# The output product of later units by seven block products for eight, their gathers moved behind it, and the clearing of one tile opened to two engines

## The chip, the cores and the metric

The kernel runs on one core of a Trainium2 chip. The metric is the device time of one execution in microseconds; a kernel's time is the median of its runs. Five engines work side by side, each through its own queue in order: TensorE (PE; its weight loads are PEld), VectorE (DVE), ScalarE (ACT), GpSimd (POOL) and SyncE (SP), which here only issues DMAs.

## The reference, cut to what matters

For each of two batches, 2048 tokens `x` (640 wide) attend to 124 text tokens (8 heads of 80), and a second branch attends through 4 adapter tokens. Both results are added, multiplied by `Wout`, and the residual is added:

```python
hs = _mha(query, keyt, valt)                       # text attention, 124 keys
ca_q1 = jnp.einsum('btc,th->bch', ca, Wq_ca)[:, indices, :]
ca_hs1 = _mha(ca_q1, residual, residual)           # 384 distinct queries over all 2048 tokens
ca_hs2 = _mha(ca_hs1 @ Wq, ca_k2, ca_v2)           # 4 keys
out = (hs + ca_hs2) @ Wout + b_out + residual
```

`indices` repeats 384 rows over the 2048 tokens, so the second branch is computed for 384 rows only and looked up.

## The kernel before, in words

**A planner.** The body is written as generators that yield `Do(engine, fn, after, needs, frees, marks, rank)`. `Desk.run` (L122) keeps a clock for every engine, takes the operation that can start first (by its rank where several can), calls its function, which emits the instructions, and adds costs of its own. So the program's order on every engine is what this planner found. `Room` objects are counted buffers: `banks` (PSUM), `slots` (big SBUF slots), `rows` (tiles for residual rows), `ebs`, `es`, `ht2`, `ht1`, `pTs`. All arithmetic goes through a few helpers, so the profile's lines are mostly L165 (matmul), L175 (transpose), L186 (VectorE, ScalarE, GpSimd) and L206 (DMA by SP); tiles tell the groups apart.

**The work.** Tokens come in 32 tiles of 128; a unit `m` is two tiles, so there are 16 units, eight a batch.

- *Queries* (`pq`): x by Wq, 8 blocks of 512 tokens.
- *Adapter, first part* (`adapter`, L1158): per batch 24 sets of scores `s1` (tiles `s`), each reduced to maxima by one long VectorE instruction into `mx`. Then a tile `mt` is cleared on POOL (L1198), the maxima of `mx` are reduced into it, transposed by PE (`pm`), added to `ca0` and split into `cop`. With `cop` known, 32 more sets of scores (`s`) follow, each with an exponential on ScalarE (`ea`) and a contraction on PE (`acc`).
- *Adapter, second part* (`second`, L1293): from `acc` to `o2`, 384 rows of 640 in HBM per batch: the second branch, already multiplied by Wout and with the bias.
- *Text scores and softmax* (`text_scores` L1402, `softmax` L1435): per tile, scores `sc`, maxima `m`, differences into `p`, exponential, sum `r`, quotient (on POOL or VectorE), a 32x32 transpose `eb` on VectorE, and a store to HBM (`kept`).
- *Output of a unit* (`probabilities` L1490, `text_out` L1590): four loads bring the probabilities back with keys on partitions (`pT`); PE multiplies them by the values (`ph`, in three groups: head parts 0 and 1, 2 and 3, the rest), ScalarE or VectorE copies them out (`hsT` or `ht_more`, five chunks of 128 rows by 256 tokens), and PE multiplies them by `Wout`: for each of two tiles and each half of the 640 columns, five products of 128x128 by 128x320 into one bank `po`. So a unit has 20 products. `added` (L1666) adds `po` to the row tile (`xo` or `x_more`), which holds the residual.
- *Rows* (`residual` L1560, `add_second` L1580): the residual rows are loaded into a row tile. If `o2` is known when they are loaded, a gather on POOL adds the rows of `o2` at once, ahead of the unit's products; otherwise (`early`) the gather comes behind the adds; and if `o2` is still unknown there, the sum is stored to HBM, loaded again later (`xp`, `x_more`) and gathered then. A gather is an indirect DMA with an add; POOL writes its descriptors.

**Spare room.** When the last queries are done, `spread_out` (L1519) gives the big slots that came free to new buffers: a second `pT`, two more `eb`, more `hsT` (`ht_more`), two more probability tiles `p_more`, four more row tiles (`x_more`).

**Matmul records.** A product of float32 operands shows as two records in the profile: the 640 records of `po` are 16 units of 20 products.

Of the kernel before, what the change touches and what calls it, by code (L numbers as in the profile page):

```python
# [212 lines left out]
def kernel(  # L213
# [944 lines left out]
    def adapter(b):  # L1158
# [36 lines left out]
        both, at = op.value, op.slots[0][0]  # L1195
        mt = both[:, :2].rearrange("p j (a k) -> p a j k", a=NCC)
        less = both[:, 2:]
        yield Do("POOL", lambda: desk.g_memset(mt, 0.0))  # L1198

        def spread():  # L1200
            for k in (MAX, MAX + 1):
# [190 lines left out]

    kept_of, xr_of, early = {}, {}, {}

    def tiles(m):

# [91 lines left out]
    def probabilities(m):  # L1490

# [26 lines left out]

    def spread_out():  # L1519

        op = yield Do("NONE", lambda z: z[0], [("q", len(blocks) - 1)], needs=[(slots, 1)])
        spare["pT"] = op.value
        pTs.at.append(op.at.t)

        def more_eb(z):
            t = slot(z[0], "eb_more", [P, 2, 4 * HEADS * R])
            more_of.append(t.rearrange("p z (j h a) -> p z j h a", j=4, h=HEADS))

        op = yield Do("NONE", more_eb, [("q", len(blocks) - 1)], needs=[(slots, 1)])
        ebs.at += [op.at.t] * 2  # L1530

        def another_ht(z):
            t = slot(z[0], "ht_more", [P, 5 * 2 * P])
            more_ht[2] = [t[:, 4 * P * i : 4 * P * (i + 1)] for i in range(2)]
            more_ht[1] = [t[:, 8 * P :]]

        op = yield Do("NONE", another_ht, [("q", len(blocks) - 1)], needs=[(slots, 1)])
        ht2.at += [op.at.t] * 2
        ht1.at += [op.at.t]
        op = yield Do(  # L1540
            "NONE", lambda z: slot(z[0], "p_more", [P, 2, HEADS, NTOK]), [("q", len(blocks) - 1)], needs=[(slots, 1)]
        )
        more = op.value

        def clear():
            for i in range(2):
                desk.g_memset(more[:, i, :, NK:], 0.0)
                late["e"].append(more[:, i])

        op = yield Do("POOL", clear)  # L1550
        es.at += [op.at.t] * 2
# [6 lines left out]
        rows.at += [op.at.t] * 4  # L1558

    def residual(m):  # L1560

        xr = xr_of[m] = []
        for b, st in tiles(m):

            def load(at):
                t = x_tile(at[0], f"xo_{b}_{st}")
                dma(t, x[b, st * P : (st + 1) * P, :], 1.3)
                return t

# [20 lines left out]
    def text_out(m):  # L1590

        N = 2 * P
        b = tiles(m)[0][0]
        rank = lambda: 30 + m if desk.known(("o2", b)) else 60 + m
        for c0, n in ((0, 2), (2, 2), (4, 1)):

            def product(s, z, c0=c0, n=n):
                pT = pT_of[m]
                ph = bank(s[0], f"ph_{m}_{c0}")
                for k in range(n):  # L1600
                    for h in (2 * (c0 + k), 2 * (c0 + k) + 1) if c0 < 4 else ():
                        half = slice(VH * (h % 2), VH * (h % 2 + 1))
                        matmul(
                            ph[half, k * N : (k + 1) * N], vpad[b][:, h, :VH],
                            pT[:, :, :, h, :].rearrange("p i k a -> p k i a"),
                            start=True, stop=True, skip_group_check=True,
                        )
                for h in (0, 2, 4, 6, 1, 3, 5, 7) if c0 == 4 else ():
                    part = slice(R * (h // 2), R * (h // 2 + 1))
                    matmul(  # L1610
                        ph[part, :N], vpad[b][:, h, VH:],
                        pT[:, :, :, h, :].rearrange("p i k a -> p k i a"),
                        start=(h % 2 == 0), stop=(h % 2 == 1), skip_group_check=True,
                    )
                return ph

            room = ht2 if n == 2 else ht1
            op = yield Do(
                "PE", product, [("pT", m), "v done"], needs=[(banks, 1), (room, 1)],
                frees=[(pTs, room_of["pT", m])] if c0 == 4 else [],  # L1620
                mode=(P, 64 if c0 < 4 else 32), rank=rank,
            )
            room_of["hsT", m, c0] = room, op.slots[1][0]

            def out_of(ph=op.value, z=op.slots[1][0], n=n, c0=c0):
                if z >= 2:
                    t = more_ht[n][z - 2]
                else:
                    t = late["pool"].tile([P, n * N], F32, tag=f"ht{n}{z}", name=f"hsT_{m}_{c0}")
# [33 lines left out]

    hs_of = {}

    def added(m, k, u, po, s, at):  # L1666

        b, st = tiles(m)[k]
# [27 lines left out]
        if early[m]:  # L1696
# [70 lines left out]
```

## Time and profile before

| | us |
|---|---|
| time, median of 3 runs | 666.96 (666.58 to 667.25) |
| the profiled execution's own time | 666.84 |
| its span, first to last instruction | 665.1 |
| TensorE busy | 640.8 |
| VectorE busy | 395.0 |
| ScalarE busy | 207.8 |
| GpSimd busy | 119.2 |

How to read the lines below. A group line has the line of code, engine, operation, output <- input, shapes, count, then busy us and mean ns of one, then the idle time of the engine ahead of these instructions and what ended it. A timeline line has start, length, engine, what, and in brackets the idle time ahead of it and its releaser. The chain of waits is followed back from the last instruction. A DMA line has the size of one and the median time from issue to landing. Busy spans of PE overlap, since matmuls are pipelined: for what one costs, count a long run of them. In the table by stretches a bracket behind a busy time is the number of instructions.

### The profile page before, as it was taken

How to read it: one execution, taken by the hardware profiler on the slowest of the kernel's cores; microseconds unless marked ns; L12 is line 12 of the kernel's file. 1: busy time of each engine (PE TensorE's matmuls, PEld its weight loads, DVE VectorE, ACT ScalarE, POOL GpSimd, SP SyncE). 2: the span in 40 equal slices, each digit the busy share in tenths (PEclk: the TensorE clock that was granted, in tenths of full speed). 3: DMA queues.
4: the chain of work that ended last, by engine and by line, in shares of the span. 5: the costliest groups of instructions: out<-in, count | busy, mean ns of one | idle time of the engine just before them, and what ended most of it. 6: DMA issues, size and time to landing. Idle time of an engine off the chain costs nothing.

```text
span 665.1 us, 9016 instructions
## 1 busy us (share of the span) xinstructions
PE 640.8 (96%) x3547; PEld 319.6 (48%) x3547; DVE 395.0 (59%) x556; ACT 207.8 (31%) x264; POOL 119.2 (18%) x174
## 2 busy tenths in 40 slices
PE   6999999999999999999998999969999999999997
PEld 4555443344453433334444455544444456665665
DVE  2368999999998756978999999621010031111111
ACT  2221322322125665524332321105655632101010
POOL 7120101202026010001201108232020000126030
PEclk9999999999999999999999999969999999999999
DMA  8898359468274335231245288999191138599981
GB/s 271 144 235 117 72 159 226 122 165 166 79 163 97 131 98 109 89 102 33 83 124 162 90 199 218 256 251 228 49 248 43 45 98 203 203 228 276 284 235 59
DMA packets 135556, 102.39 MB, mean 154 GB/s; under 512 B 78293, under 2 KB 107349, under 8 KB 135514
## 3 DMA queue, kind: packets, MB, share of 16 engines
q1 hardware_dynamic: 129882, 91.13, 52.3%
q0 software_dynamic: 5632, 10.69, 8.8%
q8 instruction: 28, 0.46, 0.3%
q14 instruction: 14, 0.11, 0.1%
HBM read 64.30 MB, written 37.49 MB: 153 GB/s over the span
## 4 chain that ended last, share of the span: by engine, by line
PE 72%; DVE 20%; issue 3%; DMA 2%; POOL 1%; SPq 1%; ACT 0%; DVEq 0%; POOLq 0%
PE po L165 24%; PE pq L165 20%; PE acc L165 7%; PE ph L165 5%; DVE mx L186 5%; PE s L165 5%; PE sc L165 5%; DVE r L186 3%; DVE m L186 3%; DVE p L186 2%; DVE eb L186 2%; PE pyz L165 2%; DMA out_dram<-xo 2%; PE pk L165 1%; PE pv L165 1%
## 5 line engine op out<-in xcount | busy, mean ns | idle before, releaser
L165 PE MATMUL pq<-xt,wq_sb 128*128 128x512 f32 x320 | 154.6, 609 | 1.8 <-DVE p L186 0.8
L186 ACT ACTIVATE ea<-s 128x1536 f32<-128x1536 f32 x64 | 92.8, 1450 | 95.2 <-PE s L165 95.2
L165 PE MATMUL po<-wout_sb,hsT 128*128 128x320 f32 x376 | 119.2, 447 | 0.5 <-ACT hsT L186 0.5
L186 DVE TENSOR_REDUCE mx<-s 128x4 f32<-128x2048 f32 x48 | 109.1, 2273 | 7.0 <-PE s L165 6.7
L165 PEld LDWEIGHTS pq<-xt,wq_sb 128*128 128x128 f32 x320 | 55.7, 189 | 72.9 <-issue 70.6
L165 PEld LDWEIGHTS po<-wout_sb,hsT 128*128 128x128 f32 x376 | 69.8, 193 | 42.0 <-issue 17.1
L186 POOL TENSOR_TENSOR p<-p,r 128x992 f32<-128x992 f32 x19 | 35.4, 1861 | 282.5 <-DVE r L186 282.5
L165 PE MATMUL po<-wout_sb,ht_more 128*128 128x320 f32 x264 | 83.8, 442 | 0.0
L186 DVE TENSOR_TENSOR xo<-xo,po 128x320 f32<-128x320 f32 x36 | 17.3, 481 | 95.0 <-PE po L165 95.0
L186 DVE TENSOR_TENSOR x_more<-x_more,po 128x320 f32<-128x320 f32 x28 | 13.6, 486 | 89.7 <-PE po L165 89.7
L165 PEld LDWEIGHTS po<-wout_sb,ht_more 128*128 128x128 f32 x264 | 48.2, 190 | 29.9 <-issue 7.8
L165 PE MATMUL acc<-ea,y_sb 128*32 128x384 f32 x512 | 54.6, 498 | 0.0
L186 ACT ACTIVATE p<-p 128x992 f32<-128x992 f32 (+1 forms) x32 | 31.5, 985 | 65.8 <-DVE p L186 65.6
L1582 POOL DMA_INDIRECT x_more<-o,query x17 | 26.2, 1542 | 140.9 <-DMA x_more<-early 87.8
L165 PE MATMUL ph<-pT,vpad 128*32 128x256 f32 (+1 forms) x512 | 48.9, 386 | 1.1 <-issue 0.7
L186 DVE TENSOR_REDUCE m<-sc 128x4 f32<-128x496 f32 x64 | 42.0, 657 | 12.6 <-PE sc L165 12.6
L186 DVE TENSOR_TENSOR p<-sc,m 128x496 f32<-128x496 f32 x60 | 40.5, 674 | 2.1
L165 PEld LDWEIGHTS sc<-kmain,q 64*128 64x128 f32 x512 | 31.5, 187 | 17.3 <-issue 15.3
L165 PE MATMUL pq<-xt,wq 128*128 128x512 f32 x80 | 39.6, 609 | 0.0
L186 DVE TENSOR_REDUCE r<-p 128x8 f32<-128x992 f32 (+1 forms) x32 | 35.7, 1116 | 5.8 <-ACT p L186 5.8
L186 ACT COPY q<-pq 128x512 f32<-128x512 f32 x34 | 19.8, 584 | 58.2 <-PE pq L165 58.2
L165 PE MATMUL sc<-kmain,q 64*128 64x124 f32 x512 | 37.1, 284 | 0.0
(175 smaller groups left out, 566.6 us busy)
## 6 DMA issues: line engine op xcount, KB each, us to landing
pT<-kept SPq DMA_DIRECT2D x64, 256.0 KB, 7.2
kept<-eb SPq DMA_DIRECT2D x28, 512.0 KB, 3.5
xi<-in_x_dram SPq DMA_DIRECT2D x28, 256.0 KB, 4.6
xo<-in_x_dram SPq DMA_DIRECT2D x18, 320.0 KB, 7.5
out_dram<-x_more SPq DMA_DIRECT2D x17, 320.0 KB, 2.5
x_more<-in_x_dram SPq DMA_DIRECT2D x14, 320.0 KB, 6.6
out_dram<-xo SPq DMA_DIRECT2D x13, 320.0 KB, 5.9
y<-yt SPq DMA_DIRECT2D x16, 256.0 KB, 2.9
```

What stands on the lines that cost most here:

```text
L165: self.pin(self.nc.tensor.matmul(out, lhsT, rhs, **kw))
L186: self.pin(getattr(engine, what)(*args, **kw))
L1582: desk.pin(nc.gpsimd.indirect_dma_start(out=t, out_offset=None, in_=o2_of[b], in_offset=bass.IndirectOffsetOnAxis(ap=query[:, st : st + 1] ...
```

## The change

Three edits, of which the first two hang together.

1. **Seven block products.** From the unit that starts after four sums of blocks of `Wout` are made (`wsum`), `text_out` hands over to `text_out_fast`. The first four of the five chunks are taken as 2 x 2 blocks: tokens of tile 0 and tile 1 by chunks 0-1 and 2-3, and `Wout` as chunks 0-1 and 2-3 by column halves. By Winograd's scheme the four blocks of the result come from seven block products (each two PE products) in place of eight; the fifth chunk keeps its four products. So a unit has 18 products. It needs four sums of `hs` blocks (`s1` to `s4`, 128x256 each, on VectorE or POOL) and, once, four sums of `Wout` blocks of 128x640 on VectorE. The products are kept in four chains, each in one PSUM bank. After each step of a chain VectorE adds the bank to one of the four blocks of the result, and the next step goes on accumulating in the same bank: four, two, one and one steps, so eight adds a unit for four.
2. **Gathers last.** `early` becomes `gather_last`, true for every unit but the last: the gather of `o2` follows the adds and stands ahead of the store.
3. **The maxima's tile.** The clearing of `mt` may go to VectorE or POOL (the planner takes the one that is free first), with rank 0.

`spread_out` hands its slots out differently: four more row tiles, the sums of `Wout`, two sets `hs` (which replace the `hsT` buffers for these units) and the second `pT`. The two more `eb`, the `ht_more` and the `p_more` are gone: one `eb` and two `p` remain.

```diff
-        yield Do("POOL", lambda: desk.g_memset(mt, 0.0))
+        def clear():
+            (desk.g_memset if desk.engine == "POOL" else desk.v_memset)(mt, 0.0)
+
+        yield Do(("DVE", "POOL"), clear, rank=0)
...
+        def sums_of_wout(z):
+            t = slot(z[0], "wout_sums", [P, 4, 2, HALF])
+            w = [[wout_sb[:, 2 * k : 2 * k + 2, u * HALF : (u + 1) * HALF] for u in range(2)] for k in range(2)]
+            for i, (x, y) in enumerate(
+                ((w[0][1], w[0][0]), (w[1][1], t[:, 0]), (w[1][1], w[0][1]), (w[1][0], t[:, 1]))
+            ):
+                desk.v_tensor_tensor(t[:, i], x, y, ALU.subtract)
...
+        yield Do("DVE", sums_of_wout, [("q", len(blocks) - 1)], needs=[(slots, 1)], marks=["wsum"], rank=4)
...
-        ebs.at += [op.at.t] * 2
...
-        early[m] = not desk.known(("o2", b))
-        if early[m]:
+        gather_last[m] = m < UNITS - 1 or not desk.known(("o2", b))
+        if gather_last[m]:
...
+        if desk.known("wsum"):
+            yield from text_out_fast(m, rank)
+            return
...
+    def text_out_fast(m, rank):
...
+        a = [[hs[:, 2 * k : 2 * k + 2, i * P : (i + 1) * P] for k in range(2)] for i in range(2)]
+        last = [hs[:, 8, i * P : (i + 1) * P] for i in range(2)]
+        s1, s2, s3, s4 = [hs[:, 4 + i].rearrange("p (c t) -> p c t", c=2) for i in range(4)]
+        of1 = [("hsT", m, 0)]
+        of2 = of1 + [("hsT", m, 2)]
+        for name, to, x, y, op, after in (
+            ("s3", s3, a[0][0], a[1][0], ALU.subtract, of1), ("s1", s1, a[1][0], a[1][1], ALU.add, of2),
+            ("s2", s2, s1, a[0][0], ALU.subtract, [("hs", m, "s1")]),
+            ("s4", s4, a[0][1], s2, ALU.subtract, [("hs", m, "s2")]),
+        ):
...
+            yield Fork(one(Do(("DVE", "POOL"), sums, after, marks=[("hs", m, name)], rank=1)), 1)
...
+        chains = (
+            (((a[0][0], w[0][0], None), one_h, ((0, 0),)), ((s2, t2, None), [("hs", m, "s2")], ((1, 0),)),
+             ((s1, t1, None), [("hs", m, "s1")], ((0, 1),)), ((None, None, (1, 1)), end_h, ((1, 1),))),
+            (((s3, t3, None), [("hs", m, "s3")], ((1, 1),)), ((a[1][1], t4, (1, 0)), both_h + end_h, ((1, 0),))),
+            (((a[0][1], w[1][0], (0, 0)), both_h + end_h, ((0, 0),)),),
+            (((s4, w[1][1], (0, 1)), [("hs", m, "s4")] + end_h, ((0, 1),)),),
+        )
...
+                def product(s=None, k=k, x=x, y=y, plus=plus):
+                    to = bank(s[0], f"po_{m}_{n}") if s else po
+                    pairs = [(x[:, c], y[:, c]) for c in range(2)] if x is not None else []
+                    if plus:
+                        pairs.append((last[plus[0]], five[plus[1]]))
+                    for c, (l, r) in enumerate(pairs):
+                        matmul(
+                            to[:, :HALF], l, r, start=(k == 0 and c == 0), stop=(c == len(pairs) - 1),
+                            skip_group_check=True,
+                        )
+                    return to
...
+                def add(i=i, u=u, po=po):
+                    t = xr_of[m][i][0][:, u * HALF : (u + 1) * HALF]
+                    desk.v_tensor_tensor(t, t, po[:, :HALF], ALU.add)
+
+                op = yield Do("DVE", add, [op.at], frees=[(banks, s)] if end else [], rank=1)
+                at = [op.at]
```

**What the change moves.** Units 2 to 15 take the new way (fourteen units). Up to the multiply of the softmax of tile 11 of batch 1 the orders agree on PE and VectorE; they part there.

POOL, at the clearing of `mt` of batch 1, before. `mt_1` is the tile, rows with DMA are gathers into row tiles (`xo`, `x_more`), `o2_0` is the second branch of batch 0:

```order
L1582 DMA x_more_2894<-o2_0_2607,query_116 128x640 x2
L1582 DMA xo_0_4_2783<-o2_0_2607,query_116 128x640
L1582 DMA x_more_2894<-o2_0_2607,query_116 128x640
L1582 DMA xo_0_5_2785<-o2_0_2607,query_116 128x640
L1582 DMA xo_0_9_3023<-o2_0_2607,query_116 128x640
L186 MEMSET mt_1_3087 128x3x2x128
L1582 DMA x_more_2894<-o2_0_2607,query_116 128x640
```

And of the change (`hs_1` and `hs_0` are the `hs` sets of the units; p_1 is a probability tile):

```order
L186 TENSOR_TENSOR p_0_693<-p_0_693,r_1_14_2957 128x8x124
L1575 DMA xo_0_4_2807<-o2_0_2607,query_116 128x640
L186 TENSOR_TENSOR hs_1_2796<-hs_1_2796 128x256 x2
L1575 DMA x_more_2758<-o2_0_2607,query_116 128x640
L186 TENSOR_TENSOR hs_1_2796<-hs_1_2796 128x256
L186 MEMSET mt_1_3112 128x3x2x128
L1575 DMA x_more_2758<-o2_0_2607,query_116 128x640 x2
L186 TENSOR_TENSOR hs_0_2795<-hs_0_2795 128x256
```

The clearing is POOL's in both. Before, the gather right ahead of it is that of a row tile of unit 4 (`xo_0_9`), which comes ahead of that unit's adds; now the gathers ahead of it are those of unit 2, which follow the unit's adds, with sums of unit 3 between.

VectorE, at the last maxima of batch 1 (`mx`, from the scores `s1_1_3`), up to their reduction into `mt`, before:

```order
L186 TENSOR_REDUCE mx_1_1913<-s1_1_3_1_1_3013 128x4
L186 TENSOR_TENSOR xo_0_5_2785<-xo_0_5_2785,po_0_5_0_3008 128x320
L186 TENSOR_REDUCE mx_1_1913<-s1_1_3_2_0_3031 128x4
L186 TENSOR_TENSOR xo_0_5_2785<-xo_0_5_2785,po_0_5_1_3025 128x320
L186 TENSOR_REDUCE mx_1_1913<-s1_1_3_2_1_3054 128x4
L186 TENSOR_REDUCE mt_1_3087<-mx_1_1913 128x3x2x4 x2
```

And of the change (`po_3_n` is chain n of unit 3, `eb_15_1` the transposed probabilities of the last tile):

```order
L186 TENSOR_TENSOR x_more_2758<-x_more_2758,po_3_1_3073 128x320
L186 TENSOR_REDUCE mx_1_1913<-s1_1_3_2_0_3014 128x4
L186 TENSOR_TENSOR x_more_2758<-x_more_2758,po_3_2_3080 128x320
L186 TENSOR_TENSOR x_more_2758<-x_more_2758,po_3_3_3087 128x320
L186 TENSOR_TENSOR x_more_2758<-x_more_2758,po_3_0_3063 128x320
L186 TENSOR_REDUCE mx_1_1913<-s1_1_3_2_1_3098 128x4
L186 TENSOR_TENSOR x_more_2758<-x_more_2758,po_3_1_3073 128x320
L186 STREAM_TRANSPOSE eb_15_1_3114<-p_1_694 128x1024
L186 TENSOR_REDUCE mt_1_3112<-mx_1_1913 128x3x2x4 x2
```

Adds of unit 3 now stand among the last reductions, and one of them and the last transpose of the softmax between the last `mx` and the reduction into `mt`; before, adds of unit 2 stood singly between reductions, and none of this behind the last.

PE, the products of the last unit, before (a bank `po_1_14_0` is one tile and one half of the columns, five products each):

```order
L165 MATMUL po_1_14_0_4272<-wout_sb_104,hsT_15_2_4247 128x320
L165 MATMUL po_1_14_0_4272<-wout_sb_104,ht_more_2759 128x320
L165 MATMUL po_1_14_1_4282<-wout_sb_104,hsT_15_0_4243 128x320 x2
L165 MATMUL po_1_14_1_4282<-wout_sb_104,hsT_15_2_4247 128x320 x2
L165 MATMUL po_1_14_1_4282<-wout_sb_104,ht_more_2759 128x320
L165 MATMUL po_1_15_0_4289<-wout_sb_104,hsT_15_0_4243 128x320 x2
L165 MATMUL po_1_15_0_4289<-wout_sb_104,hsT_15_2_4247 128x320 x2
L165 MATMUL po_1_15_0_4289<-wout_sb_104,ht_more_2759 128x320
L165 MATMUL po_1_15_1_4297<-wout_sb_104,hsT_15_0_4243 128x320 x2
L165 MATMUL po_1_15_1_4297<-wout_sb_104,hsT_15_2_4247 128x320 x2
L165 MATMUL po_1_15_1_4297<-wout_sb_104,ht_more_2759 128x320
```

And of the change (`po_15_0` to `po_15_3` are the four chains, `ph` the hidden values, `wout_sums` the sums of `Wout` blocks):

```order
L165 MATMUL ph_15_2_4315<-pT_15_4208,vpad_1_112 64x256 x4
L165 MATMUL po_14_0_4274<-wout_sb_104,hs_0_2795 128x320
L165 MATMUL ph_15_4_4323<-pT_15_4208,vpad_1_112 32x256 x8
L165 MATMUL po_15_0_4336<-wout_sb_104,hs_1_2796 128x320 x2
L165 MATMUL po_15_1_4342<-wout_sums_2771,hs_1_2796 128x320 x2
L165 MATMUL po_15_2_4346<-wout_sb_104,hs_1_2796 128x320 x3
L165 MATMUL po_15_3_4351<-wout_sb_104,hs_1_2796 128x320 x3
L165 MATMUL po_15_0_4336<-wout_sums_2771,hs_1_2796 128x320 x2
L165 MATMUL po_15_1_4342<-wout_sums_2771,hs_1_2796 128x320 x2
L165 MATMUL po_15_1_4342<-wout_sb_104,hs_1_2796 128x320
L165 MATMUL po_15_0_4336<-wout_sums_2771,hs_1_2796 128x320 x2
L165 MATMUL po_15_0_4336<-wout_sb_104,hs_1_2796 128x320
```

The last unit has 18 products for 20, and a chain's bank is come back to after the adds: chain 0 in the first, fifth, eighth and ninth of the rows `po_15`. Its last two steps stand next to each other, since nothing is left to put between them.

More of the change, by code (lines that the diff above doesn't have):

```diff
@@ L1391 @@
     late_sq = sq_stack.enter_context(tc.tile_pool(name="ps_sq", bufs=1, space=bass.MemoryType.PSUM))
-    kept_of, xr_of, early = {}, {}, {}
+    kept_of, xr_of, gather_last = {}, {}, {}
     def tiles(m):
@@ L1482, in eb_tile @@
     def eb_tile(i, name):
-        if i:
-            return more_of[0][:, i - 1]
         return late["pool"].tile([P, 4, HEADS, R], F32, tag="eb", name=name)
-    more_of, more_ht = [], {}
+    wsum, hs_sets, hss = [], [], Room(0)
     def probabilities(m):
@@ L1519, in spread_out @@
     def spread_out():
[L1521 to L1529, printed above, removed]
-        ebs.at += [op.at.t] * 2
[L1532 to L1551, printed above, removed]
         def another_row(z):
@@ L1558, in spread_out, with another_hs @@
         rows.at += [op.at.t] * 4
+        def sums_of_wout(z):
[5 more added lines that the diff above has]
+                desk.v_tensor_tensor(t[:, i], x, y, ALU.subtract)
+            wsum.extend(t[:, i] for i in range(4))
+        yield Do("DVE", sums_of_wout, [("q", len(blocks) - 1)], needs=[(slots, 1)], marks=["wsum"], rank=4)
+        for i in range(2):
+            def another_hs(z):
+                hs_sets.append(slot(z[0], f"hs_{i}", [P, 10, 2 * P]))
+            op = yield Do("NONE", another_hs, ["wsum"], needs=[(slots, 1)])
+            hss.at.append(op.at.t)
+        op = yield Do("NONE", lambda z: z[0], [("q", len(blocks) - 1)], needs=[(slots, 1)])
+        spare["pT"] = op.value
+        pTs.at.append(op.at.t)
     def residual(m):
@@ L1594, in text_out @@
         rank = lambda: 30 + m if desk.known(("o2", b)) else 60 + m
+        if desk.known("wsum"):
+            yield from text_out_fast(m, rank)
+            return
         for c0, n in ((0, 2), (2, 2), (4, 1)):
             def product(s, z, c0=c0, n=n):
[L1598 to L1615, printed above, removed]
+                return hidden(m, c0, n, bank(s[0], f"ph_{m}_{c0}"))
             room = ht2 if n == 2 else ht1
@@ L1625, in out_of @@
             def out_of(ph=op.value, z=op.slots[1][0], n=n, c0=c0):
[L1626 to L1629, printed above, removed]
+                t = late["pool"].tile([P, n * N], F32, tag=f"ht{n}{z}", name=f"hsT_{m}_{c0}")
                 copy(t, ph[:, : n * N])
@@ L1664, with hidden @@
     hs_of = {}
+    def hidden(m, c0, n, ph):
+        N = 2 * P
+        b = tiles(m)[0][0]
+        pT = pT_of[m]
+        for k in range(n):
+            for h in (2 * (c0 + k), 2 * (c0 + k) + 1) if c0 < 4 else ():
+                half = slice(VH * (h % 2), VH * (h % 2 + 1))
+                matmul(
+                    ph[half, k * N : (k + 1) * N], vpad[b][:, h, :VH],
+                    pT[:, :, :, h, :].rearrange("p i k a -> p k i a"),
+                    start=True, stop=True, skip_group_check=True,
+                )
+        for h in (0, 2, 4, 6, 1, 3, 5, 7) if c0 == 4 else ():
+            part = slice(R * (h // 2), R * (h // 2 + 1))
+            matmul(
+                ph[part, :N], vpad[b][:, h, VH:],
+                pT[:, :, :, h, :].rearrange("p i k a -> p k i a"),
+                start=(h % 2 == 0), stop=(h % 2 == 1), skip_group_check=True,
+            )
+        return ph
@@ L1666, in added @@
+    fast_of, tile_left, ends = {}, {}, {}
     def added(m, k, u, po, s, at):
@@ L1677, in added, with stored @@
         )
-        if u == 0:
-            return
+        if u:
+            yield from stored(m, k, [("added", m, k, 0), op.at])
+    def stored(m, k, both):
+        b, st = tiles(m)[k]
         t, i, _ = xr_of[m][k]
         rows_out = out[b, st * P : (st + 1) * P, :]
-        both, own = [("added", m, k, 0), op.at], []
-        if early[m] and not desk.known(("o2", b)):
+        own = []
+        if gather_last[m] and not desk.known(("o2", b)):
             part = hbm.tile([P, H], F32, tag=f"early_{m}_{k}", name=f"early_{b}_{st}")
@@ L1695, in added @@
             both = [op.at]
-        if early[m]:
+        if gather_last[m]:
             op = yield Do("POOL", lambda: add_second(t, b, st), [*both, ("o2", b), "query"])
```

49 lines of the change are left out of this document (added).

## The prediction

> **What bounds the kernel now.** I read the page first: the engines' totals, the slices and the chain that ended last by engine.
>
> ```profile
> span 665.1 us, 9016 instructions
> PE 640.8 (96%) x3547; PEld 319.6 (48%) x3547; DVE 395.0 (59%) x556; ACT 207.8 (31%) x264; POOL 119.2 (18%) x174
> PE   6999999999999999999998999969999999999997
> DVE  2368999999998756978999999621010031111111
> PEclk9999999999999999999999999969999999999999
> PE 72%; DVE 20%; issue 3%; DMA 2%; POOL 1%; SPq 1%; ACT 0%; DVEq 0%; POOLq 0%
> ```
>
> TensorE is the bound over the run, VectorE beside it up to slice 26; behind that VectorE is nearly free. One slice stands out on TensorE and on its clock. The table by stretches of time shows it:
>
> ```profile
> 380.00:410.00 30.00, 28.80 (x196) 16.33 (x195) 29.52 (x39) 7.05 (x10) 10.78 (x8) 1.00 0.78 192
> 410.00:420.00 10.00, 9.48 (x45) 5.68 (x46) 9.14 (x9) 0.59 (x1) 6.19 (x4) 1.00 1.03 259
> 420.00:440.00 20.00, 12.81 (x89) 7.03 (x88) 7.40 (x9) 2.50 (x5) 6.83 (x5) 0.85 1.01 257
> 440.00:450.00 10.00, 10.00 (x34) 6.57 (x33) 2.40 (x4) 2.05 (x2) 1.62 (x2) 0.78 1.08 245
> 600.00:640.00 40.00, 40.00 (x211) 25.45 (x210) 5.85 (x12) 4.63 (x9) 18.30 (x12) 1.00 1.03 276
> ```
>
> Columns: stretch, busy time of PE, PEld, DVE, ACT, POOL, then granted clock, DMA share, GB/s. Before 420 DVE is full; from 420 to 440 PE loses 7.2 us and clock; later PE is full again. The timeline says why:
>
> ```profile
> 425.73 2.29 DVE L186 TENSOR_REDUCE mx<-s 128x4 f32<-128x2048 f32 x1 [0.91 <-PE s L165]
> 427.62 1.88 PE L165 MATMUL po<-wout_sb,hsT 128*128 128x320 f32 x6
> 431.08 0.70 PE L165 MATMUL po<-wout_sb,ht_more 128*128 128x320 f32 x2
> 436.09 1.54 POOL L1582 DMA_INDIRECT xo<-o,query  x1 [9.46 <-issue]
> 437.04 1.33 POOL L186 MEMSET mt<- 128x768 f32 x1
> 438.97 0.87 PE L175 MATMUL pm<-ident,mt 128*128 128x128 f32 x3 [7.19 <-DVE mt L186]
> 439.64 3.41 PE L165 MATMUL po<-wout_sb,hsT 128*128 128x320 f32 x6
> ```
>
> The last maxima are reduced at 428.0, but `mt` is cleared only at 437.04, behind a gather that stood 9.46 us at the head of POOL's queue; PE meets the transposes `pm` in its fixed order and waits 7.19 us. A like run of six took 1.88 us before the wait and 3.41 after it: 1.53 us of slow clock there.
>
> **Products: eight blocks become seven.** A long run of pure output products gives the price of one matmul record:
>
> ```profile
> 553.71 22.82 PE po L165 x84
> ```
>
> 22.82 / 84 = 0.272 us. A product in the code is two records (the 640 `po` records are 16 units of 20 products), so 0.543 us. The program's order shows units 2 to 15, fourteen units, with 18 products for 20: 28 x 0.543 = 15.2 us less on the engine that sets the end.
>
> **The stall.** `mt` is still cleared by POOL, so the either-engine edit by itself moves nothing. But the gathers ahead of it no longer wait for a row's load: they wait for adds on VectorE that lie well ahead of the last reduction (one 1.54 us gather, one sum and the 1.33 us clear follow an add that has some 11 us of VectorE work between it and the reduction into `mt`). So I take 7.2 us of wait and the slow clock as gone. The slow clock I price at 2.6 us: 10 x 0.22 = 2.2 from the stretch 440 to 450, and some 0.4 for the microsecond at half clock ahead of it (1.53 of it is the row's). A rule on this: the Trainium skill ("TensorE: Matmul & The Clock Gate", the HAM clock gate) lets PE go to half clock after an idle window of 3.4 us and back after as long a busy one, so it would price the restart at 3.4 x 1/2 = 1.7 us and the sum 0.9 us later. The trace agrees on the kind (half speed behind a wait of 7.19 us); on the size its rows go first.
>
> **VectorE up to the transposes.** The stage from 381.6, where the two orders part, has new work for a full VectorE. Its prices:
>
> ```profile
> L186 DVE TENSOR_REDUCE mx<-s 128x4 f32<-128x2048 f32 x48 | 109.1, 2273 | 7.0 <-PE s L165 6.7
> L186 DVE TENSOR_REDUCE m<-sc 128x4 f32<-128x496 f32 x64 | 42.0, 657 | 12.6 <-PE sc L165 12.6
> L186 DVE TENSOR_TENSOR p<-sc,m 128x496 f32<-128x496 f32 x60 | 40.5, 674 | 2.1
> L186 DVE TENSOR_REDUCE r<-p 128x8 f32<-128x992 f32 x30 | 35.2, 1173 | 5.4 <-ACT p L186 5.4
> L186 DVE STREAM_TRANSPOSE eb<-p 128x1024 f32<-128x1024 f32 x27 | 33.2, 1229 | 0.2
> L186 DVE TENSOR_TENSOR xo<-xo,po 128x320 f32<-128x320 f32 x36 | 17.3, 481 | 95.0 <-PE po L165 95.0
> L186 DVE RECIPROCAL r<-r 128x8 f32<-128x8 f32 x32 | 6.5, 203 | 1.1
> L186 DVE TENSOR_REDUCE mt<-mx 128x24 f32<-128x96 f32 x4 | 0.8, 237 | 10.4 <-POOL mt L186 10.4
> 381.60 1.19 DVE L186 TENSOR_TENSOR p<-p,r 128x992 f32<-128x992 f32 x1
> ```
>
> The line through 496 elements (0.674) and 992 (1.19) gives 0.16 us + 1.04 ns an element: 0.82 us for a sum over 640, 0.42 for one over 256. Between the multiply at 381.60 and the last `mx`, VectorE had eight `mx` (18.2), eight pairs of `m` and `p` (10.6), four `r` with their reciprocals (5.5), five `eb` (6.1), eight adds (3.8), the multiply and a copy (1.8): 46.0 us, in 46.4 of time. In the changed order the same stretch has four sums over 640 (+3.3), nine more adds (+4.3), one more multiply (+1.2) and one sum (+0.4), one `eb` less (-1.2): 54.0 us, at the same density 54.5, so the last `mx` would end at 436.1. One add, the fifth `eb` (0.5 + 1.2) and the two short reductions into `mt` (0.5) follow: `pm` at about 438.4, against 438.97. TensorE has ten more products by that place (5.4 us; 55 of units 1 to 15 for 45) and one group `ph_4_4` less (1.1), on the 50.6 us that it took without its wait (381.2 to 438.97, less 7.19): 54.9 us, so 436.1. The two lean on one another, and I take 439.5, half a microsecond later than now. Of the products 217 are left then, where 255 were; with `ph_4_4` still to come, 38 x 0.543 - 1.1 = 19.6 us less to do.
>
> **Adds and sums behind that.** Each unit has eight adds for four (+4 x 0.48) and four sums (1.7): 3.6 us more in a unit's 13 on an engine that is busy 6 us in 40 there. What counts is whether PE waits. These rows price an exposed handshake and a unit's rhythm:
>
> ```profile
> 626.85 1.95 PE L165 MATMUL ph<-pT,vpad 128*64 128x256 f32 x16
> 628.73 2.96 PE L165 MATMUL po<-wout_sb,hsT 128*128 128x320 f32 x10
> 631.61 1.07 PE L165 MATMUL ph<-pT,vpad 128*32 128x256 f32 x16
> 634.77 1.54 POOL L1582 DMA_INDIRECT x_more<-o,query  x1 [0.31 <-issue]
> 660.76 0.70 PE L165 MATMUL po<-wout_sb,ht_more 128*128 128x320 f32 x2
> 661.50 0.49 DVE L186 TENSOR_TENSOR x_more<-x_more,po 128x320 f32<-128x320 f32 x1 [2.21 <-PE po L165]
> ```
>
> The add starts 0.04 us after the product's end and takes 0.49; with some 0.1 back (my estimate), a chain's next step can go 0.65 us after the last. In the order at least three products (1.6 us) or two `ph` groups stand between two steps of a chain, except in the last unit, where the last step follows at once: +0.7 us at the tail, once. The sum that POOL makes for a unit can stand behind one gather: add 0.5, gather 1.54 + 0.31, sum 0.5, so 2.9 us after the product that released the gather. PE comes to it after both `ph` groups and three products with their switches (1.9 + 1.0 + 3 x 0.54 + 0.3 = 4.8): 1.9 us of slack.
>
> **Buffers and queues.** The transposed probabilities have one buffer `eb` where three were, and SP's queue has stores that now wait for gathers, with the loads of `pT` behind them. Landings, us, from 400 to 450 and from 600 on:
>
> ```profile
> kept<-eb_more SPq DMA_DIRECT2D x3, 512.0 KB, 16.1
> kept<-eb SPq DMA_DIRECT2D x1, 512.0 KB, 6.6
> x_more<-o,query POOLq DMA_INDIRECT x5, 10.1
> pT<-kept SPq DMA_DIRECT2D x8, 256.0 KB, 12.8
> ```
>
> The five transposes into `eb` stand 11 to 14 us apart. A landing of 6.6 costs nothing; one of 16.1 makes VectorE wait 16.1 + 0.5 (its issue) - 12 = 4.6, four times at most: 0 to 18 us. The stores are spread further apart than the ones that took 16.1 (two issued back to back among other transfers), so I stay near the low end: +2. A `pT` behind a gather's store is late by 10.1, and has two buffers, so over a unit (13 us) of lead: nothing. A gather last also delays only stores; the last unit gathers first, and the gather of unit 14 has a unit's time: nothing.
>
> **The sum.** The profiled execution took 666.84 us (span 665.1 and 1.74 around it), 0.12 under the median of 666.96. 666.84 + 0.5 (`pm` later) - 19.6 - 2.6 + 0.7 (tail) + 2 (`eb`) = 647.8; small waits I cannot place stay in the range; **648**. This one's own range: 643.5 (no `eb` wait, `pm` 2 us sooner) to 653 (5 us of new waits).
>
> **Rivals.**
> - *The single `eb` buffer with full DMA becomes the bound of the stage before `pm`.* For it: DMA share above 1.0 from 410 to 440 and the 16.1 us. Against: fewer bytes are asked for at once. With 4.6 us at two to four transposes: 655 to 664; 658 as a middle. Chance 0.20.
> - *The clear of `mt` stays late*, since POOL still makes it and the edit that allows VectorE does nothing. For it: the same queue, with gathers and sums ahead. Against: none of those waits for a load. 7.2 + 2.6 back: 657.6. Chance 0.08.
> - *VectorE and POOL hold each other up before `pm`.* VectorE has seven instructions with both inputs in SBUF there, POOL multiplies of this kind:
>
> ```profile
> L186 POOL TENSOR_TENSOR p<-p,r 128x992 f32<-128x992 f32 x19 | 35.4, 1861 | 282.5 <-DVE r L186 282.5
> 405.25 2.44 POOL L186 TENSOR_TENSOR p_more<-p_more,r 128x992 f32<-128x992 f32 x1
> ```
>
>  Each meeting half of a multiply, 7 x 0.93 = 6.5: 654.5. One multiply of 2.44 for 1.86 speaks for it; against it, VectorE's 46.0 us of work filled 46.4 us of time with four such multiplies beside it. Chance 0.04. The Trainium skill ("SBUF — State Buffer", on the shared port pair) states such an exclusive lock for a VectorE instruction with two SBUF inputs against a GpSimd one; the 2.44 us is all that this trace shows of it.
> - *Slower: the steps of a chain lie open.* Each of 14 units has four places where PE reads on after an add. If other products do not cover them, each costs 0.65 and a switch of 0.3, about 0.95. The whole gain of 19 us is gone at 20 such places; two a unit are 26.6 us: 674. Against: 1.6 us of cover by the order. Chance 0.06.
>
> The range takes in the first two rivals' middles: **642 to 660**; beyond it lie the worse part of the `eb` case, the slower case and a little below. 0.2% (1.3 us) is about what a measurement of this kernel tells from no change. All but the last rival are faster by more; chances 0.92 faster, 0.02 within, 0.06 slower.
>
> **What would show it.** Right: 28 x 2 = 56 fewer `po` records at an unchanged 0.272; no wait over 1 us ahead of `pm`, no slice with a lower clock, `pm` at 437 to 442; PE full from there to the last unit. Wrong: VectorE waiting for `kept<-eb` (the first rival), POOL's clear ending after the last `mx` (the second), PE idle with a VectorE add or POOL sum as releaser in each unit (the last).

## The result, and the profile after

The changed kernel took 644.69 us (median of 4 runs, 644.59 to 647.32) beside 666.79 for the kernel before (4 runs): ratio 0.9677 [0.9652, 0.9702]. Fourteen runs in all, in three sets, lie from 644.03 to 647.85, with medians of 644.69, 646.35 and 646.06; of the second set 644.7 within 1.3 was expected, so it came out 0.35 us above that. Forecast were 648.0 us and a range of 642 to 660. The profiled execution took 644.6 us, 3.2 less than the sum's 647.8.

The page of the changed kernel, the lines that stood in the prediction for the kernel before:

```profile
span 642.9 us, 9088 instructions
PE 625.1 (97%) x3491; PEld 306.9 (48%) x3491; DVE 440.8 (69%) x657; ACT 207.7 (32%) x263; POOL 132.1 (21%) x188
PE   6999999999999999999999999999999999999997
DVE  2459999999998785796999999995222224333333
PEclk9999999999999999999999999999999999999999
PE 69%; DVE 23%; DMA 4%; issue 2%; POOL 1%; SPq 1%; ACT 0%; DVEq 0%; POOLq 0%
```

The slice with a 6 on PE and on its clock is gone, and PE has 56 records fewer. VectorE is busy 45.8 us more, and behind slice 26, where it was nearly free, it is full for one slice more and then stands at 2 to 5. The chain of waits has more of DMA (4% for 2%). The stretch ahead of and at the transposes `pm`:

```profile
420.00:440.00 20.00, 19.61 (x121) 11.71 (x118) 18.87 (x31) 3.99 (x6) 9.39 (x9) 1.00 1.06 279
```

From 420 to 440 PE has 19.61 us of work where it had 12.81, at full clock, and VectorE 18.87 where it had 7.40. The timeline there:

```profile
400.33 0.50 PE L165 MATMUL s<-zop,cop 32*128 32x512 f32 x4 [1.50 <-DVE mx L186]
427.61 0.73 POOL L186 MEMSET mt<- 128x768 f32 x1
431.18 2.28 DVE L186 TENSOR_REDUCE mx<-s 128x4 f32<-128x2048 f32 x1
434.57 1.25 DVE L186 STREAM_TRANSPOSE eb<-p 128x1024 f32<-128x1024 f32 x1 [0.72 <-DMA kept<-eb]
436.26 0.52 PE L175 MATMUL pm<-ident,mt 128*128 128x128 f32 x3 [0.39 <-DVE mt L186]
```

The clear now lies 5 us ahead of the last maxima, the one wait for the `eb` buffer is 0.72 us, and PE waits 0.39 us at `pm`. Its longest wait in the stage is the 1.50 us for VectorE at 400.33. The groups of the new work:

```profile
L165 PE MATMUL po<-wout_sb,hs 128*128 128x320 f32 x280 | 89.0, 445 | 0.6 <-DVE xo L186 0.6
L165 PE MATMUL po<-wout_sums,hs 128*128 128x320 f32 x224 | 70.4, 441 | 0.1
L186 DVE TENSOR_TENSOR wout_sums<-wout_sb,wout_sums 128x640 f32<-128x640 f32 x2 | 1.6, 822 | 0.0
L186 DVE TENSOR_TENSOR hs<-hs 128x256 f32<-128x256 f32 x39 | 16.4, 423 | 22.6 <-ACT hs L186 11.9 <-POOL hs L186 9.6
L186 POOL TENSOR_TENSOR hs<-hs 128x256 f32<-128x256 f32 x17 | 15.6, 951 | 31.7 <-ACT hs L186 31.1 <-DVE hs L186 0.5
```

280 + 224 records are the 14 units with 36 each, and PE sat idle 0.7 us ahead of all of them together: the steps of the chains do not wait, except once in the last unit. VectorE's prices are the forecast ones (0.82 and 0.42); GpSimd's sum is not (0.95 for 0.5).

### The profile page after: what moved, and what is told of

Read it like the earlier page. It is cut to its first block, busy times and chain, and to the rows that moved or that the text cites. A ratio compares the mean times of both kernels' runs of the same rounds, so it can differ in the third digit from the quotient of the medians.

```text
span 642.9 us, 9088 instructions
## 1 busy us (share of the span) xinstructions
PE 625.1 (97%) x3491; PEld 306.9 (48%) x3491; DVE 440.8 (69%) x657; ACT 207.7 (32%) x263; POOL 132.1 (21%) x188
## 3 DMA queue, kind: packets, MB, share of 16 engines
q1 hardware_dynamic: 129882, 91.13, 53.2%
## 4 chain that ended last, share of the span: by engine, by line
PE 69%; DVE 23%; DMA 4%; issue 2%; POOL 1%; SPq 1%; ACT 0%; DVEq 0%; POOLq 0%
PE pq L165 20%; PE po L165 19%; PE acc L165 7%; DVE mx L186 7%; PE sc L165 5%; PE s L165 5%; PE ph L165 5%; DVE r L186 3%; DVE m L186 3%; DVE p L186 3%; DVE eb L186 2%; DMA xo<-in_x_dram 2%; PE pyz L165 2%; DMA kept<-eb 2%; PE pk L165 1%
## 5 line engine op out<-in xcount | busy, mean ns | idle before, releaser
L186 POOL TENSOR_TENSOR p<-p,r 128x992 f32<-128x992 f32 x20 | 37.8, 1889 | 275.8 <-DVE r L186 275.8
L165 PE MATMUL po<-wout_sb,hs 128*128 128x320 f32 x280 | 89.0, 445 | 0.6 <-DVE xo L186 0.6
L165 PE MATMUL po<-wout_sums,hs 128*128 128x320 f32 x224 | 70.4, 441 | 0.1
L186 DVE TENSOR_TENSOR x_more<-x_more,po 128x320 f32<-128x320 f32 x60 | 28.6, 485 | 58.3 <-PE po L165 50.1
L165 PEld LDWEIGHTS po<-wout_sb,hs 128*128 128x128 f32 x280 | 50.3, 189 | 33.3 <-issue 9.1
L186 DVE TENSOR_TENSOR xo<-xo,po 128x320 f32<-128x320 f32 x60 | 28.8, 482 | 53.2 <-PE po L165 52.0
L186 ACT COPY hs<-ph 128x512 f32<-128x512 f32 (+1 forms) x40 | 20.7, 517 | 105.8 <-PE ph L165 105.6
L165 PEld LDWEIGHTS po<-wout_sums,hs 128*128 128x128 f32 x224 | 40.8, 190 | 25.2 <-issue 7.5
L186 DVE TENSOR_REDUCE m<-sc 128x4 f32<-128x496 f32 x64 | 42.1, 658 | 13.3 <-PE sc L165 13.3
L186 DVE TENSOR_TENSOR p<-sc,m 128x496 f32<-128x496 f32 x64 | 43.2, 674 | 2.2
L186 DVE STREAM_TRANSPOSE eb<-p 128x1024 f32<-128x1024 f32 x32 | 39.4, 1231 | 0.9 <-DMA kept<-eb 0.7
```

Of the source, the lines that this page charges most:

```text
L165: self.pin(self.nc.tensor.matmul(out, lhsT, rhs, **kw))
L186: self.pin(getattr(engine, what)(*args, **kw))
```

## The experiments

**The gathers alone.** The kernel before with one line of the second edit:

```diff
-        early[m] = not desk.known(("o2", b))
+        early[m] = m < UNITS - 1 or not desk.known(("o2", b))
```

> The kernel before with the second edit alone: gathers behind the adds in every unit but the last, 20 products a unit, the buffers of before, the clear of mt still only on POOL. Theory (the gather that waited for a row's load was what held the clear, and the stall cost 7.2 us of wait and 2.6 us of slow clock): the wait ahead of pm is gone, time 666.8 - 9.8 = 657.0, within 1.5. Rival (the clear stays late behind the gathers that now wait for adds): pm still waits several us and the time is 663 to 667.

Measured: 658.71 us, ratio 0.9885 [0.9869, 0.9902]. Its timeline:

```profile
425.56 1.54 POOL L1582 DMA_INDIRECT xo<-o,query  x1 [5.09 <-DVE xo L186]
426.20 2.29 DVE L186 TENSOR_REDUCE mx<-s 128x4 f32<-128x2048 f32 x1 [0.91 <-PE s L165]
426.52 1.33 POOL L186 MEMSET mt<- 128x768 f32 x1
430.90 0.55 PE L175 MATMUL pm<-ident,mt 128*128 128x128 f32 x3
```

The clear ends 0.6 us ahead of the last `mx`; PE reaches `pm` without a wait. The mechanism is as forecast, the worth is 7.6 us and not 9.8.

**The either-engine clear alone.** The kernel before with the third edit:

```diff
-        yield Do("POOL", lambda: desk.g_memset(mt, 0.0))
+        def clear():
+            (desk.g_memset if desk.engine == "POOL" else desk.v_memset)(mt, 0.0)
+
+        yield Do(("DVE", "POOL"), clear, rank=0)
```

> The kernel before with the third edit alone: the clear of mt may go to VectorE or POOL. In the program's order VectorE makes it for batch 1, right behind the last mx. The prediction said of this edit that by itself it moves nothing: 666.8. Theory now: the cover for the stall is the same whichever way the clear is taken out from behind the gather, so 657, with pm some 1 us behind the last mx. Both edits that reach the clear would then be worth the same 9.8 us, and not together 19.6.

Measured: 659.13 us, ratio 0.9893 [0.9877, 0.991]. VectorE clears, right behind the last `mx`:

```profile
428.13 0.70 DVE L186 MEMSET mt<- 128x768 f32 x1
429.43 0.52 PE L175 MATMUL pm<-ident,mt 128*128 128x128 f32 x3
430.86 0.49 PE L175 MATMUL pm<-ident,mt 128*128 128x128 f32 x3
431.19 1.78 PE L165 MATMUL po<-wout_sb,hsT 128*128 128x320 f32 x6
432.90 1.07 PE L165 MATMUL ph<-pT,vpad 128*32 128x256 f32 x16
```

So this edit does move something where the gathers stand first: alone it is worth 7.2 us. In the whole change it moves nothing, since the changed program with the clear on POOL alone has the same order on every engine. These rows also give the slow clock by itself: six records of `po` take 1.71 us to the next start here (431.19 to 432.90). In the kernel before, where the granted clock is 0.50 from 438 to 444, behind the rows at 438.97 and 439.64 that the prediction shows, stand

```profile
442.84 0.85 PE L175 MATMUL pm<-ident,mt 128*128 128x128 f32 x3
443.48 1.11 PE L165 MATMUL po<-wout_sb,hsT 128*128 128x320 f32 x2
444.43 0.70 PE L165 MATMUL po<-wout_sb,ht_more 128*128 128x320 f32 x2
```

so six records take 3.20 there (439.64 to 442.84). With 0.67 for 0.35 at the first `pm`, 0.64 for 0.33 at the second and 0.95 for 0.64 at the next two records, the slow clock cost 2.4 us.

**No seven products.** The changed kernel with the old products in every unit (`if False:` ahead of `text_out_fast`), so both other edits and the new division of the buffers:

> The changed kernel with the old 20 products in all units: gathers last, clear by either engine, one eb and two p as in the change, and the four sums of Wout still made. Theory (product count is worth 28 x 0.543 = 15.2 us, less the tail's 0.6): 644.7 + 14.6 = 659.3; with the four sums still on VectorE, 657 to 660. Rival (the fewer buffers cost several us by themselves and hide in the changed kernel's gain): above 662. Rival (the sums and adds cost PE several us, so that seven products are worth less than counted): below 656.

Measured: 659.35 us, ratio 0.9907 [0.9889, 0.9925]. The seven products are worth 659.35 - 644.69 = 14.7 us, or 13.0 to 13.3 by the later medians of the changed kernel; the smaller buffers, and the four sums of `Wout` that this kernel still makes, cost nothing that shows beside the two kernels above.

**Seven products alone.** The changed kernel with gathers first where `o2` is known, and the clear on POOL alone (the line of the gathers):

```diff
-        gather_last[m] = m < UNITS - 1 or not desk.known(("o2", b))
+        gather_last[m] = not desk.known(("o2", b))
```

> The changed kernel with the gathers ahead of the products again wherever o2 is known, and the clear only on POOL: seven products alone. Theory (the two gains add): the wait ahead of pm comes back in full with its slow clock, 644.7 + 9.8 = 654.5. Rival (VectorE, fuller by 5 us in that stage, ends its last mx so late that the clear is hidden): 645 to 648.

Measured: 670.97 us, ratio 1.0073 [1.0048, 1.0098]: 4.7 us slower than the kernel before, and neither of the two expectations. Not the clear (PE waits 1.1 us at `pm`); the largest wait of PE is in the tail:

```profile
608.71 1.54 POOL L1575 DMA_INDIRECT xp<-o,query  x1 [8.43 <-DMA xp<-early]
610.99 1.54 POOL L1575 DMA_INDIRECT xo<-o,query  x1 [0.73 <-DMA pT<-kept]
622.20 1.68 DVE L186 TENSOR_TENSOR xo<-xo,po 128x320 f32<-128x320 f32 x4 [16.18 <-DMA xo<-o,query]
622.74 2.50 PE L165 MATMUL po<-wout_sums,hs 128*128 128x320 f32 x4 [14.68 <-DVE xo L186]
```

A gather stands at POOL behind one that waits 8.43 us for a reload; issued at 610.99, it has its row ready only at 622.2, 11.2 us later. VectorE's add has waited 16.18 us for it, and PE, whose next chain step may not go on in the bank before that add has read it, 14.68. With 20 products no matmul reads on behind an add, and the same gathers hold up only the freeing of banks. PE's waits from 381 to 600 were 10.7 us (2.6 in the changed kernel), behind 600 15.9 (0.6).

**Gathers first in batch 0 alone.** As the last, but `gather_last[m] = UNITS // 2 <= m < UNITS - 1 or ...`:

> Seven products, the clear only on POOL, and the gathers ahead of the products in batch 0 alone; in batch 1 they come last as in the changed kernel. Seven products with gathers ahead everywhere took 671: PE's waits were 10.7 us from 381 to 600 there (2.6 in the changed kernel) and 15.9 behind 600 (0.6), with a slow clock behind them. Theory (each batch's own gathers make its waits, since PE's next step waits for an add and the add for the gathered row): the 15.3 us and the slow clock behind 600 go, the 8 us before stay: 652 to 654. Rival (the tail's wait is backlog from batch 0): 665 and more. Rival (batch 0's gathers cost nothing): 645 to 647.

Measured: 657.72 us, ratio 0.9878 [0.9848, 0.9909]. Between the theory and the first rival: the tail's long wait is gone, as the theory has it, but 4.6 us of waits are left behind 600, and one new wait lies ahead of `pm`:

```profile
434.06 2.99 PE L165 MATMUL po<-wout_sb,hs 128*128 128x320 f32 x6 [1.94 <-POOL hs L186]
```

This row also shows a slow clock, behind a wait of only 1.94 us: six records take 2.99 us for the 1.88 of a like row, with a granted clock of 0.67 from 434 to 436 and 0.50 from 436 to 438. By such rows it costs 1.7 us. PE's waits are 9.0 us from 381 to 600 and 4.6 behind, 10.4 us more than in the changed kernel's first profile. Together that is 12.1 of the 13.1 us between the two profiled runs (657.66 and 644.6). So the theory's own part, 8 us up to 600, measured 6.5, and the rest is the 4.0 us of waits in the tail and the slow clock that it had not counted. Why the tail's rows come late in this order was not settled.

**VectorE's load up to `pm`.** The changed kernel with every sum of `Wout` made twice; the planner is told the cost of one, in lines not shown, so that the order on all engines stays:

```diff
                 desk.v_tensor_tensor(t[:, i], x, y, ALU.subtract)
+                desk.v_tensor_tensor(t[:, i], x, y, ALU.subtract)
...
```

> The changed kernel with each of the four sums of Wout made twice, one right after the other, in an otherwise unchanged order on every engine. That is 4 x 0.82 = 3.3 us more on VectorE between its multiply at 381.9 and the last mx. Theory (VectorE sets when pm comes, as its rows have only 1.1 us of idle there): last mx at 433.5 + 3.3 = 436.7, pm at 439.5, and PE, which waits for VectorE's mx and mt there for 1.9 us in the changed kernel, waits 3 us longer, so the time is 647 to 648. Rival (PE's own work sets pm at 436): pm by 437 and the time unchanged within 0.8.

Measured: 650.65 us (649.04 to 655.58), beside 646.35 for the changed kernel in the same set, ratios 0.9774 [0.9748, 0.98] and 0.9692 [0.9674, 0.971]. The timeline:

```profile
390.94 1.85 PE L165 MATMUL sc<-kmain,q 64*128 64x124 f32 x13 [3.19 <-DVE p L186]
434.65 2.29 DVE L186 TENSOR_REDUCE mx<-s 128x4 f32<-128x2048 f32 x1
439.41 0.52 PE L175 MATMUL pm<-ident,mt 128*128 128x128 f32 x3
```

Last `mx` and `pm` come 3.5 and 3.2 us later, as the theory has it, and the time goes up by 4.3 (3.25 between the two profiled runs, 649.6 and 646.35); the 647 to 648 were missed, since they stood on 644.7. The place of the wait is not the expected one: PE waits 3.19 us early, at 390.94, with a slow clock behind it (0.50 from 392 to 394), and not at all at `pm` or where the changed kernel waits 1.50. The order and PE's work are the same in both kernels, so it is VectorE's load that moved `pm`. The two engines come to it together: in the three profiles of the changed kernel PE waits there for 0.39, 0 and 0.18 us.

**The sums on GpSimd.** The same four sums by `g_tensor_tensor`, as an operation of POOL:

> The changed kernel with the four sums of Wout on GpSimd and not VectorE. Theory (VectorE sets pm, so 3.3 us off it are worth what PE waits there, 1.9 us, and no more, since PE's own work then sets the time): 642.8, with no PE wait over 0.5 us between 381 and 440. Rival (the sums, four of some 1.3 us by the rate of GpSimd's multiplies, hold up the softmax's multiplies or the two engines hold each other up): 645 to 650.

Measured: 645.13 us (642.68 to 648.46), ratio 0.9692 [0.9671, 0.9713]: no difference from the changed kernel that the runs can tell. The theory's 642.8 is not the median; its condition holds, since in the profiled run (642.68) no wait of PE from 381 to 440 reaches 0.5 us, and together they are 0.7 for 1.5 to 1.9. The median lies in the rival's range, but no wait that it names shows. `pm` comes at 432.42, which is not VectorE's doing alone: the planner found another order, with 106 records of `po` ahead of `pm` for 110 and 96 of `ph` for 104. GpSimd's rate for such a sum:

```profile
373.78 1.55 POOL L186 TENSOR_TENSOR wout_sums<-wout_sb 128x640 f32<-128x640 f32 x1
```

1.54 us for VectorE's 0.82, 1.9 times as long. The Trainium skill ("GPSIMD Engine Reference", 3.1 Elementwise) has about twice for a float32 add; the trace agrees.

**The exposed step of the last unit.** In the changed kernel's tail:

```profile
637.86 0.49 DVE L186 TENSOR_TENSOR xo<-xo,po 128x320 f32<-128x320 f32 x1 [0.59 <-PE po L165]
638.40 0.81 PE L165 MATMUL po<-wout_sb,hs 128*128 128x320 f32 x2 [0.58 <-DVE xo L186]
```

```diff
+        if m == UNITS - 1:
+            own = ((None, None, (1, 1)), end_h, ((1, 1),))
+            chains = (chains[0][:3], *chains[1:3], (own,), chains[3])
+            left["products"] += 1
```

> The changed kernel with one edit in the last unit: the fifth chunk's product of the block of tile 1 and the second half, which stood as last step of chain 0 behind an add, gets a bank of its own and goes ahead. Theory (the exposed handshake at the tail costs the 0.58 us that PE waits for the add, and no more): PE's last record ends 0.6 us sooner, span 642.3, time 644.1. Rival (what ends last is a store to the output, not PE): the span moves by less than 0.3 us.

In this kernel the last block lacks chain 0's sum; the adds are eight, as many as before. Measured: 645.26 us, ratio 0.9675 [0.9663, 0.9688]. Its span is 644.6, that of the changed kernel beside it 644.5: the rival's number, though not by its cause, since PE waits 0.9 us longer for late row loads in units 13 and 14 of this run (2.8 for 1.9). The tail itself is shorter: PE's wait of 0.58 is gone. In the changed kernel of that set, and then in this one:

```profile
632.30 3.39 PE L165 MATMUL po<-wout_sb,hs 128*128 128x320 f32 x12
640.04 0.81 PE L165 MATMUL po<-wout_sb,hs 128*128 128x320 f32 x2 [0.58 <-DVE xo L186]
640.88 0.49 DVE L186 TENSOR_TENSOR x_more<-x_more,po 128x320 f32<-128x320 f32 x1 [0.90 <-PE po L165]
```

```profile
633.17 3.93 PE L165 MATMUL po<-wout_sb,hs 128*128 128x320 f32 x14
639.63 1.24 PE L165 MATMUL po<-wout_sums,hs 128*128 128x320 f32 x4
640.91 0.49 DVE L186 TENSOR_TENSOR xo<-xo,po 128x320 f32<-128x320 f32 x1 [0.59 <-PE po L165]
```

From 632.30 to the last add at 640.88 are 8.58 us, from 633.17 to 640.91 7.74: the exposed step costs 0.84.

**Every step exposed.** Chains 0 and 1 of each unit emitted as one piece, each step followed by its bank's add:

```diff
+        def at_once(n, steps):
...
-            yield Fork(chain(n, steps), 30 + m)
+            yield Fork((chain if n > 1 else at_once)(n, steps), 30 + m)
```

> The changed kernel with chains 0 and 1 of every unit put on TensorE as one piece: each step of these two chains follows its own bank's add with nothing between. That opens 14 x 4 = 56 places where PE reads on after an add, for one in the changed kernel. Theory (each open place costs the 0.58 us that the last unit's place shows): 55 x 0.58 = 32 us more, 677. The prediction's slower rival (0.65 and a switch of 0.3, so 0.95 a place): 697. Rival (VectorE's adds come late in a busy stage, so that a place costs more up to pm): over 700.

Measured: 728.76 us, ratio 1.0928 [1.091, 1.0946]: the last rival's number, over 700, but not its cause, since PE's waits at these places are 0.58 to 0.77 us ahead of `pm` and behind it alike. Steps of one chain, and the ends of PE and of POOL:

```profile
654.82 1.34 PE L165 MATMUL po<-wout_sums,hs 128*128 128x320 f32 x4 [0.58 <-DVE xo L186]
656.84 1.32 PE L165 MATMUL po<-wout_sums,hs 128*128 128x320 f32 x4 [0.67 <-DVE xo L186]
658.73 0.81 PE L165 MATMUL po<-wout_sb,hs 128*128 128x320 f32 x2 [0.58 <-DVE xo L186]
...
677.32 3.93 PE L165 MATMUL po<-wout_sb,hs 128*128 128x320 f32 x14
...
719.24 1.54 POOL L1575 DMA_INDIRECT xp<-o,query  x1 [6.73 <-DMA xp<-early]
```

A step of four records takes 2.02 and 1.89 us from start to start, for 4 x 0.272 = 1.09: 0.8 to 0.9 a place. PE ends at 681.2, the changed kernel's PE at 639.2: 42 us for 55 places, 0.76 each, between the theory's 0.58 and the prediction's 0.95. Behind PE's end lie 46.4 us, where the changed kernel has 3.7, so the other 42.7 us come there: `pm` is at 471.7 in this kernel, so `o2` of batch 1 comes later, more rows are stored early and loaded again, and POOL's last gather waits for such a load. That part belongs to the order this kernel got, not to the chains.

**Both small edits together**: sums on GpSimd, and the last unit's fifth chunk in its own bank with chain 0's sum added to both blocks (nine adds).

> The changed kernel with two edits: the four sums of Wout on GpSimd, and in the last unit the fifth chunk's product of the block of tile 1 and the second half in a bank of its own, with chain 0's sum added to two blocks (nine adds for eight), so that no step waits behind an add. Theory: 0.8 us at the tail less one add of 0.41, and some 1.2 us of PE's waits up to pm, so 1.6 us under the changed kernel. Rival (the waits for late row loads in units 13 and 14, which differ from run to run by 2 us, hide it): within 0.8 of the changed kernel.

Measured: 643.18 us (642.98 to 648.96), ratio 0.9681 [0.9647, 0.9714]; the changed kernel beside it (the set called after_third, whose expectation was the kernel's own time) 646.06 (644.03 to 647.54), ratio 0.9694 [0.9673, 0.9714]. The median is 2.9 us lower, but the intervals lie on each other: whether it is faster is open. They spread by 3.5 and 6 us, where the kernel before spreads by 2 (665.4 to 667.4 in one set). A wait that changes between runs of the changed kernel is that for the row loads of units 13 and 14; in the second set's profile:

```profile
620.49 0.49 DVE L186 TENSOR_TENSOR x_more<-x_more,po 128x320 f32<-128x320 f32 x1 [5.04 <-DMA x_more<-in_x_dram]
621.03 1.34 PE L165 MATMUL po<-wout_sums,hs 128*128 128x320 f32 x4 [0.77 <-DVE x_more L186]
622.99 1.68 DVE L186 TENSOR_TENSOR x_more<-x_more,po 128x320 f32<-128x320 f32 x4 [2.02 <-DMA x_more<-in_x_dram]
623.53 1.34 PE L165 MATMUL po<-wout_sums,hs 128*128 128x320 f32 x4 [1.16 <-DVE x_more L186]
```

PE loses 1.9 us there; in the first profile no wait of PE at that place reaches 0.5 us. That these loads make the whole spread is argued, not shown.

## Why the prediction was right, and where its sizes were off

*Products, 15.2 us: right.* 56 fewer records, and 13.0 to 14.7 us between the kernels with and without seven products; 15.2 less the exposed step's 0.84 is 14.4.

*The stall, 7.2 + 2.6 us: mechanism right, net worth less.* The wait is gone, by the gathers as forecast; the slow clock of 2.6 measured 2.4 in rows. The half-clock rule of the Trainium skill ("TensorE: Matmul & The Clock Gate") would have made that 1.7; the rows decide for 2.4. The idle window of 3.4 us that the prediction quotes from it does not fit the kernel with gathers first in batch 0, where half clock follows a wait of 1.94 us. But the kernels with this gain alone are only 7.2 and 7.6 us faster. In the one with the clear on VectorE PE's last record ends at 652.96 for 661.46, 8.5 sooner, and from there to the end of the span are 4.3 us for 3.6. So 0.7 goes to what follows PE; 1.1 is lost on PE behind `pm`, where the program has 140 runs of matmuls into one kind of tile for 131. That the nine more changes make it was not tested. The sum counted the stall at its full size.

*The two edits hang together.* The prediction gave "gather last" only the stall. With 20 products its place is worth 7.6 us (666.3 to 658.7), with seven 671.0 - 645 = 26: the chains need it, since each step waits for an add and the add for a gathered row. The prediction named the add as the only link ("each costs 0.65 and a switch of 0.3") and left out what the add itself waits for. The forecast didn't need it, since it was for both edits together.

*VectorE up to `pm`: the step that was mis-sized.* It put 54.0 us of work "at the same density" as before, last `mx` at 436.1 and `pm` at 439.5. Measured: 433.46 and 436.26. The work was counted right (the rows of the stretch sum to 53.8); the density was not constant. The group of the maxima in that stretch, in the kernel before and in the changed one:

```profile
L186 DVE TENSOR_REDUCE mx<-s 128x4 f32<-128x2048 f32 x8 | 18.2, 2278 | 2.4 <-PE s L165 2.4
```

```profile
L186 DVE TENSOR_REDUCE mx<-s 128x4 f32<-128x2048 f32 x8 | 18.2, 2277 | 0.0
```

The 46.4 us held 2.4 us of waits for PE's scores, and the new work went into these first: 8.0 us of work cost 5.2 (381.87 to 433.46 is 51.6, with one wait of 0.7 in it). With the waits taken out first, 46.4 - 2.4 = 44.0 us for 46.0 of rows, the prediction would have had 54.0 x 44.0 / 46.0 + 0.7 = 52.3; in the last 0.7 neighbouring rows lie over one another a little more. PE's own term has the same error: its 50.6 us held 1.7 us of waits beside the 7.19. Without them the prediction's sum is 53.2, and 52.9 were measured (381.48 to 436.26, less 1.9 of waits); by its own work alone PE would have been at `pm` at 434.4, not 436.1. So VectorE binds there, by a little, and that its load moves `pm` is what making the sums twice shows.

*Behind `pm`: 19.6 + 2.6 - 0.7 forecast, 19.5 measured.* From `pm` to PE's last record were 222.5 us, now 202.95. The missing 2.0 may be of the same kind as above (142 runs for 131); late row loads make some 0.4 of it in this run. The rest was not tested.

*`eb` and queues, +2: too high.* One wait of 0.72 us, and it lies ahead of `pm`. *GpSimd's sum, 0.5: too low.* It takes 0.73 us free of other work; PE never waited for it, so the 1.9 us of slack held.

The terms together: `pm` 2.7 sooner for 0.5 later (3.2), no 2 for `eb`, 2.0 less gain behind: 3.2 us below the sum, as measured. That the `eb` term's 2 us and the 2.0 us missing behind `pm` cancel is luck.

*The signs.* Two of those that the prediction set for itself did not come: `pm` is at 436.26, not from 437 to 442, and one wait in the stage ahead of it, at 400.33, is 1.50 us, where none over 1 was to be. Both are VectorE's part, as above. The 56 records, the clock and a full PE behind `pm` came as written.

*The rivals.* `eb` as the bound, the late clear, and the two engines holding each other up did not come. The slower one has nearly the right price (0.76 to 0.9 a place for 0.95); the order leaves one such place, not 56. What the prediction took for the two engines holding each other up, a multiply of 2.44 us for 1.86, was misread. It stands right behind a gather, in the kernel before:

```profile
404.25 1.56 POOL L1582 DMA_INDIRECT x_more<-o,query  x1 [0.30 <-issue]
405.25 2.44 POOL L186 TENSOR_TENSOR p_more<-p_more,r 128x992 f32<-128x992 f32 x1
```

Its row begins while the gather still runs; from the gather's end at 405.81 to its own at 407.69 are 1.88 us, its usual time. The exclusive lock of the Trainium skill ("SBUF — State Buffer") is not tested here: VectorE's sums of two SBUF inputs keep 423 and 822 ns, but none of them runs beside a sum or multiply of GpSimd in the changed kernel's first profile.

## What to carry to other kernels

When an engine that is nearly full gets more work, its idle time is filled first: take the waits of the stretch out of the density before scaling it. When an accumulation is split into steps that read on behind another engine's add, list what that add waits for as well, and move loads and gathers behind it: a gather that held up no product before can then stop TensorE. Price an exposed step between TensorE and VectorE from start to start, not by the idle time beside it.

## What the runs showed of the hardware

A step of TensorE that waits for VectorE's add of 128x320 in its bank costs 0.76 to 0.9 us, while the profile shows 0.58 to 0.77 of idle. An instruction of GpSimd right behind a gather shows some 0.6 us too much: the clear of 128x768 takes 1.33 us behind a gather that has not ended (426.52 in the gathers' experiment) and 0.73 free of one, the 128x256 sum 1.31 for 0.73, a multiply 2.44 for 1.84. A clock of one half can follow a wait of TensorE of only 1.94 us (434.06 in the kernel with gathers first in batch 0; granted clock 0.67 and then 0.50); behind the 1.50 us at 400.33 in the changed kernel it stayed at 1.00.
